# The attention's projections under a schedule written by hand, with the order of reads, split terms and unpacking fixed around their seven products

## The chip, the cores and the metric

The kernel runs on one core of a Trainium2 chip. The metric is the device time of one execution in microseconds (us). TensorE (PE) multiplies, with its weight loads shown apart (PEld). VectorE (DVE), ScalarE (ACT) and GpSimd (POOL) do the elementwise work. SyncE (SP), ACT and POOL issue DMA transfers. Each engine works through its own queue in order.

## The reference

The input is normalised, and the normalised rows feed two branches: causal attention with rotary positions, and a gated feed-forward network whose weights are 4-bit integers with a scale and a zero per group of 128 rows. The output is the input plus the attention's result times the SiLU of the feed-forward's result. There are 2 batches of 1024 tokens, 1024 features, 32 query heads and 8 key/value heads of 32 features, and 2752 inner features. All values are fp32.

```python
def reference(x, wq, wk, wv, wo, qweight_gu, qzeros_gu, scales_gu, g_idx_gu,
              qweight_down, qzeros_down, scales_down, g_idx_down):
    xn = layernorm(x)                                     # eps 1e-5
    q, k, v = heads(xn @ wq, 32), heads(xn @ wk, 8), heads(xn @ wv, 8)
    q, k = rope(q), rope(k)                               # pairs (0::2, 1::2), theta 10000
    k, v = repeat(k, 4), repeat(v, 4)
    scores = einsum('bqhd,bkhd->bhqk', q, k) / sqrt(32) + causal_mask
    s = einsum('bhqk,bkhd->bqhd', softmax(scores), v).reshape(2, 1024, 1024) @ wo
    w_gu, w_d = dequant(qweight_gu, ...), dequant(qweight_down, ...)
    gate, up = split(xn @ w_gu, 2752)
    g = silu((silu(gate) * up) @ w_d)
    return x + s * g
# dequant: W[i, j] = scale[g[i], j] * (nibble(qw)[i, j] - (nibble(qz)[g[i], j] + 1))
```

## The kernel before

The first batch is normalised (`norm`), then each batch goes through `project` (queries, keys, values), `attend` and `project_out`; while the first batch's output projection runs, the second batch is normalised. The feed-forward network of both batches comes last (`ffn_in_order`). Two jobs run beside these stages as generators that are advanced one step at a time with `next(side, None)`. `look` belongs to the first batch's projections: it surveys scales, zeros and group indices, spreads the zeros over rows in DRAM (`zb_gu`, L218, and `zb_d`, L223, issued by ACT), and turns the scales (`scales_turned`). `unpack` turns packed weights into numbers in DRAM, one unit of 256 columns in four steps: loads by SP (L242, L244), DVE operations on `nib` (L258, L260, L263), conversions on ACT (L267), a store by POOL (L249). In the version before, units 0 to 7 of the gate and up weights are unpacked in the first output projection, 8 to 19 in the second batch's projections, and 20 and 21 with the down weights in the second output projection.

`project` forms five blocks of 256 output columns: keys (block 0), then queries (blocks 1 to 4). A block is a matrix product cut into two halves in tokens, in the summed dimension and in columns, and worked out as seven products of half-size pieces in place of eight. The weights' pieces are `wa`, `wb` and their differences (`quarters`, L397 to L400), those of the input are quarters of `xnT` and four sums `S` (L391) in the space of `oT`. `pair` writes the seven products (L431) in the order 1, 5, 2, 6, 3, 7, 4 over three PSUM banks, each read by the sums at L442, L447, L450, L451 and L457. Four results of a block are turned by `turn_heads` (rotary positions: DVE L407 and L409, POOL L410 and L411), split into a high and a low part (ACT L413, DVE L415) and stored by SP (L416, L417). The loop runs product 4 of a block behind product 1 of the next block.

`split_x` splits the normalised input the same way for the feed-forward (ACT L483, DVE L484, stores L485 and L486). `head` is the object `Maxima`: `keys()` and `queries()` load the stacks of head group 0 from the stored rotations (L594, 4 transfers, and L599, 16 transfers), and `rows()` yields 45 steps, each a product of queries and keys in one of two PSUM banks (L640, mask L634) with its row maximum on DVE (L650), then the shifts (L672 to L677) and their transposes (L685). `values` projects the values in eight tiles (L472, L475). `weights(i)` loads a block's query weights (L350), and `load_kv` the value weights (L356).

Before the change a scheduler orders the instructions of `project` on each engine, by priority in the order written and by a model of when each becomes ready; `tc.issue_after` holds some behind a rotation. `attend` has `tc.manual_schedule()`, under which every engine issues in the order in which the code writes its instructions. The names that the prediction uses: block i, its products 1 to 7, X for the end of product 5, and "step" for one yield of `rows()`.

## Time and profile before

| | us |
|---|---|
| median of 3 runs | 2316.39 (2315.3 to 2318.07) |
| the profiled execution | 2317.56 |
| its span | 2315.8 |
| PE, DVE, ACT, POOL busy in the span | 2228.9, 1501.8, 1144.4, 838.4 |
| first batch: first product of the projections to the attention's first score | 28.70 to 234.59 |
| second batch: the same | 678.77 to 873.96 |

In a row of the time order, the first number is the start in us from the span's start, the second the length, then the engine, the line, the operation and its tiles, and x the number of merged instructions; brackets hold the idle time before it and what ended it. "SPq" and "ACTq" are DMA issues in those engines' queues. An fp32 product of 512 columns leaves two records per weight tile, so a product of a block is eight records. A busy PE may still run below its peak, since its ends are modelled; the granted clock is given apart.

### The profile page before, as it was taken

To read this page: it belongs to the slowest core of one execution; us is meant where nothing else is said; L and a number is where in the kernel's file an instruction comes from. 1 tells how busy PE (TensorE), PEld (TensorE's weight loads), DVE (VectorE), ACT (ScalarE), POOL (GpSimd) and SP (SyncE) were. 2 spreads that over 40 slices of the span, in tenths; PEclk is the share of its full clock that TensorE was granted. 3 is DMA by queue.
4 is the path that set the end of the run, shared out by engine and by line. 5 is a ranking of instruction groups with operands and counts; after the bars stand their busy time and mean duration, and the time that the engine had idled before them with its cause. 6 is when DMAs were issued, how large, how long until landed. Compare 5 with 4: busy or idle time off the path is not lost.

```text
span 2315.8 us, 30821 instructions
## 1 busy us (share of the span) xinstructions
PE 2228.9 (96%) x11233; PEld 1529.2 (66%) x11233; DVE 1501.8 (65%) x2336; ACT 1144.4 (49%) x1839; POOL 838.4 (36%) x599
## 2 busy tenths in 40 slices
PE   6979999999998889999999999999999999999997
PEld 3445555555873455555548878888877888888875
DVE  8664577773336765777732367766877777777775
ACT  2102555544233324544542465555787655556875
POOL 2514667775135445777661100000234100001362
PEclk9969999999999999999999999999999999999999
DMA  6645313112477875122119632322746645333474
GB/s 191 193 145 192 85 46 85 45 48 69 141 225 218 256 231 131 46 65 64 46 38 319 222 82 55 82 77 60 264 151 221 183 132 143 91 81 102 138 233 148
DMA packets 262185, 309.52 MB, mean 134 GB/s; under 512 B 19147, under 2 KB 197707, under 8 KB 261880
## 3 DMA queue, kind: packets, MB, share of 16 engines
q1 hardware_dynamic: 245172, 260.62, 37.8%
q0 software_dynamic: 10752, 38.02, 5.3%
q10 hardware_dynamic: 6100, 8.82, 1.4%
q8 instruction: 91, 1.49, 0.3%
q14 instruction: 70, 0.57, 0.1%
HBM read 214.58 MB, written 97.03 MB: 135 GB/s over the span
## 4 chain that ended last, share of the span: by engine, by line
PE 77%; DVE 5%; POOL 5%; DMA 5%; issue 4%; ACT 2%; SPq 1%; ACTq 0%; POOLq 0%; DVEq 0%
PE acc L1284 27%; PE acc L1165 12%; PE s L640 7%; PE st L747 7%; PE ps_wo L966 6%; PE o L794 5%; PE ps L431 4%; PE l L812 3%; PE st L762 2%; DMA zt<-zb_d 2%; PE s L634 1%; POOL p L907 1%; PE ps_v L472 1%; POOL rot L410 1%; POOL rot L411 1%
## 5 line engine op out<-in xcount | busy, mean ns | idle before, releaser
L1284 PE MATMUL acc<-x,w 128*128 128x512 f32 x2752 | 639.9, 393 | 1.1 <-ACT gate L1255 0.9
L1284 PEld LDWEIGHTS acc<-x,w 128*128 128x128 f32 x2752 | 512.6, 188 | 120.0 <-DVE h L1257 7.2
L1054 DVE TENSOR_SCALAR acc<-acc,r_gu 128x1024 f32<-128x1024 f32 x301 | 389.1, 1293 | 166.1 <-PE acc L1284 164.7
L650 DVE TENSOR_REDUCE mx<-s 128x1 f32<-128x512 f32 (+3 forms) x672 | 385.0, 609 | 162.6 <-PE s L634 94.7
L772 ACT ACTIVATE p<-st 128x512 f32<-128x512 f32 (+3 forms) x768 | 315.1, 497 | 316.1 <-PE st L762 316.0
L1052 ACT ACTIVATE acc<-acc,r_gu 128x1024 f32<-128x1024 f32 x301 | 327.7, 1089 | 231.1 <-PE acc L1284 226.3
L1268 POOL TENSOR_TENSOR h_lo<-h,h_hi 128x512 fp32r<-128x512 f32 x78 | 100.3, 1287 | 805.7 <-PE acc L1165 588.2
L907 POOL TENSOR_TENSOR p<-p 128x2048 f32<-128x2048 f32 (+3 forms) x122 | 360.0, 2955 | 9.0 <-PE o L794 4.6
L1054 DVE TENSOR_SCALAR acc<-acc,r_d 128x512 f32<-128x512 f32 x320 | 241.6, 759 | 62.1 <-PE acc L1165 59.4
L1052 ACT ACTIVATE acc<-acc,r_d 128x512 f32<-128x512 f32 x320 | 211.0, 663 | 62.0 <-PE acc L1165 55.2
L966 PE MATMUL ps_wo<-oT,w_o 128*128 128x256 f32 x1024 | 232.1, 382 | 0.0
L1165 PE MATMUL acc<-h_lo,w 128*128 128x512 f32 (+1 forms) x576 | 228.9, 397 | 2.9 <-POOL h_lo L1268 2.6
L1165 PE MATMUL acc<-h_hi,w 128*128 128x512 f32 (+1 forms) x576 | 229.5, 398 | 0.7 <-ACT h_hi L1267 0.7
L966 PEld LDWEIGHTS ps_wo<-oT,w_o 128*128 128x128 f32 x1024 | 191.1, 190 | 40.9 <-issue 16.7
L794 PE MATMUL o<-p,v 128*32 128x512 f32 (+3 forms) x1536 | 162.9, 496 | 0.8 <-POOL p L775 0.8
L775 POOL TENSOR_SCALAR_AFFINE_SELECT p<-p 128x512 f32<-128x512 f32 x128 | 80.6, 637 | 160.6 <-ACT p L772 160.6
L640 PE MATMUL s<-kst,room 128*128 128x512 f32 (+3 forms) x384 | 130.5, 379 | 0.0
L1165 PEld LDWEIGHTS acc<-h_lo,w 128*128 128x128 f32 (+1 forms) x576 | 108.4, 188 | 30.7 <-POOL h_lo L1268 5.1
L1165 PEld LDWEIGHTS acc<-h_hi,w 128*128 128x128 f32 (+1 forms) x576 | 108.3, 188 | 30.6 <-issue 2.9
L747 PE MATMUL st<-room,kst 128*128 128x512 f32 (+3 forms) x384 | 119.2, 371 | 3.2 <-ACT p L772 3.2
L413 ACT CAST rot_hi<-rot 128x512 fp32r<-128x512 f32 x40 | 24.7, 617 | 177.2 <-POOL rot L411 139.0
L267 ACT ACTIVATE nf<-nib 128x1024 fp32r<-128x1024 uint8 (+2 forms) x68 | 68.2, 1040 | 88.7 <-DVE nib L263 41.3
(194 smaller groups left out, 2688.7 us busy)
## 6 DMA issues: line engine op xcount, KB each, us to landing
w<-ng SPq DMA_DIRECT2D x86, 512.0 KB
w<-nd SPq DMA_DIRECT2D x63, 512.0 KB
ng<-nf POOLq DMA_DIRECT2D x42, 512.0 KB, 6.3
room<-qs SPq DMA_DIRECT2D x160, 128.0 KB
x<-xs SPq DMA_DIRECT2D x32, 512.0 KB
qst<-qs SPq DMA_DIRECT2D x96, 128.0 KB
xt<-in_L_attn_x SPq DMA_DIRECT2D x16, 512.0 KB
w_qk<-in_L_attn_wq SPq DMA_DIRECT2D x16, 512.0 KB
```

The costliest lines, as they stand in the source:

```text
L640: nc.tensor.matmul(s[:, c * w : (c + 1) * w], q[j][:, qt * P : (qt + 1) * P], k[:, k0:k1], start=n == 1, stop=c == n - 1 and (n > 1 or not ...
L650: nc.vector.tensor_reduce(mx[:, at, js[0] : js[0] + n, k0 // TB], s[:, : w * n].rearrange("p (j t) -> p j t", j=n), AX.X, ALU.max)
L747: nc.tensor.matmul(s[:, q0:], kst[g][:, kt * P : (kt + 1) * P], stack[g][j][:, qlo + q0 : qlo + TB], start=True, stop=False,)
L772: nc.scalar.activation(p[:, j, q0:], st[j][:, q0:], AF.Exp, scale=1.0 / math.sqrt(HD))
L794: nc.tensor.matmul(o[HD * j : HD * (j + 1), q0:], v[:, kt, HD * g : HD * (g + 1)], p[:, j, q0:], start=(kt == 0), stop=last,)
L907: what(*args)
L966: self.last = nc.tensor.matmul(ps[:, c * self.BLK : (c + 1) * self.BLK], self.ws[c0 + c][:, g, :], self.oT[:, g, t0 : t0 + self.BLK], star ...
L1052: nc.scalar.mul(a, a, r)
L1054: nc.vector.tensor_scalar(a, a, r, None, ALU.mult)
L1165: nc.tensor.matmul(acc[c], w[:k, c * P : (c + 1) * P], ht[:k, :], start=(f == 0 and t == 0), stop=(t == 1), skip_group_check=(f > 0),)
L1268: nc.gpsimd.tensor_tensor(at[1][:k, :], h[:k, f, tok], at[0][:k, :].bitcast(F32), ALU.subtract)
L1284: nc.tensor.matmul(a[:, n, :], w[i][:, g * P : (g + 1) * P], xs[t][:, g, n * TB : (n + 1) * TB], start=(g == 0 and t == 0), stop=(t == 1), ...
```

## The change

`project` is put under `tc.manual_schedule()` and its instructions are written in a fixed order. The rotation's split and stores become a function `leave`, kept in a list and written one or two products later. After each product, `others()` writes the leaving rotations, one `split_x` of half a tile, and one step of the side job (before: three steps per rotation in the second batch, one in the first). The fourth weight term, on POOL, is written after product 4 of the block before. Steps of the row maxima stand at fixed places: nine per block from block 2, and three before each tile of the values. `head.keys()` and `head.queries()` are written behind product 5 of blocks 1 and 2, and the warm-up of Exp behind the last rotation. In `look`, the loads of all three parts come first, and the parts follow in the order scales and zeros, down scales and zeros, turned scales, spreading of zeros. The units of unpacking become 0 to 10 in the first output projection, 11 to 18 in the second batch's projections, and 19 to 21 with the down weights in the second output projection.

```diff
@@ survey: words, scale and idx are loaded ahead of a first yield
+        scale = pool.tile([P, 8 * w], F32, name=f"scale_{tag}")
+        nc.sync.dma_start(scale, sc.rearrange("g n -> (g n)").rearrange("(p w) -> p w", p=P))
+        idx = pool.tile([k, m], I32, name=f"idx_{tag}")
+        nc.sync.dma_start(idx, gi.rearrange("(p m) -> p m", p=k))
+        yield
...
@@ scales_turned
+        by_g = pool.tile([G_D, D], F32, name="by_g")
+        nc.sync.dma_start(by_g, sc_d)
+        yield
...
         nc.vector.tensor_copy(l_gu, ps[:, :, :, G_GU - 1 :])
-        by_g = pool.tile([G_D, D], F32, name="by_g")
-        nc.sync.dma_start(by_g, sc_d)
+        yield
...
@@ look
-        yield from survey(pool, bad, sc_gu, qz_gu, gi_gu, z_gu, 0, "gu")
-        yield from survey(pool, bad, sc_d, qz_d, gi_d, z_d, 2, "d")
+        parts = [
+            survey(pool, bad, sc_gu, qz_gu, gi_gu, z_gu, 0, "gu"),
+            survey(pool, bad, sc_d, qz_d, gi_d, z_d, 2, "d"),
+            scales_turned(pool, psp),
+        ]
+        for part in parts:
+            next(part)
+            yield
+        for part in parts:
+            yield from part
+        yield
...
-        yield
-        scales_turned(pool, psp)
         yield
@@ project
-        ) as vps, tc.tile_pool(name="x_split", bufs=2, reuse_waits="tile") as xp:
+        ) as vps, tc.tile_pool(name="x_split", bufs=2, reuse_waits="tile") as xp, tc.manual_schedule():
...
-                t = [wp.tile([P, H, P], F32, name=f"t_{i}") for i in range(3)]
+                t = [wp.tile([P, H, P], F32, name=f"t_{i}") for i in range(2)]
                 nc.vector.tensor_tensor(t[0], wb[:, low], wa[:, low], ALU.subtract)
                 nc.vector.tensor_tensor(t[1], wb[:, high], t[0], ALU.subtract)
                 nc.gpsimd.tensor_tensor(wb[:, low], wb[:, high], wb[:, low], ALU.subtract)
-                nc.gpsimd.tensor_tensor(t[2], wa[:, high], t[1], ALU.subtract)
...
+                yield B
+                B[4] = wp.tile([P, H, P], F32, name="t_2")
+                nc.gpsimd.tensor_tensor(B[4], wa[:, high], t[1], ALU.subtract)
+                yield B
...
+                nc.gpsimd.tensor_tensor(t1, t1, t2, ALU.add)
+
+                def leave():
+                    hi = pool.tile([P, TB], F32R, name="rot_hi")
+                    nc.scalar.copy(hi, t1)
+                    lo = pool.tile([P, TB], F32R, name="rot_lo")
+                    nc.vector.tensor_tensor(lo, t1, hi.bitcast(F32), ALU.subtract)
+                    nc.sync.dma_start(dst[0, :, tok], hi.bitcast(F32))
+                    nc.sync.dma_start(dst[1, :, tok], lo.bitcast(F32))
+
+                leaving.append(leave)
+
+            leaving, splits = [], []
+
+            def others(n=1):
+                while len(leaving) > n:
+                    leaving.pop(0)()
+                if splits:
+                    splits.pop(0)()
+                next(side, None)
...
-                        if s % 2 and i > 1:
+                        if i not in (1, 5) and (s == 1 or s == 3 and i != 4):
                             next(work, None)
...
                 product(5, S[0], 2, True)
                 nc.scalar.copy(p5, banks[2])
                 nc.gpsimd.tensor_tensor(p5, p1, p5, ALU.add)
+                others(0)
                 yield
                 product(2, A[0, 1], 0, False)
                 turn_heads(banks[0], 0, dsts[0])
+                others()
                 yield
                 product(6, S[1], 1, True)
                 nc.vector.tensor_tensor(u2, banks[1], p1, ALU.add)
+                others(0)
...
-            B = quarters(*loads[0])
+            make = quarters(*loads[0])
+            B = next(make)
+            for s in sums:
+                nc.vector.tensor_tensor(*s)
+            next(make)
...
                 next(g)
                 for _ in running or ():
-                    pass
+                    next(make)
+                next(g)
+
                 if i == 1:
+                    head.keys()
                     w = load_kv(None, wv, w_k)
+                if i == 2:
+                    head.queries()
                 if 0 < i < PAIRS - 1:
                     loads.append(weights(i + 1))
-                for _ in range(4):
+                if i:
+                    splits += [lambda c=c, n=n: split_x(c, n) for c in (2 * i - 2, 2 * i - 1) for n in range(NB)]
+                for _ in range(3):
                     next(g)
                 if i + 1 < PAIRS:
-                    B = quarters(*loads[i + 1])
+                    make = quarters(*loads[i + 1])
+                    B = next(make)
                 next(g)
                 running = g
-            for _ in running:
-                pass
+            next(running)
+            others(0)
+
+            warm = tp.tile([P, 1], F32, name="warm")
+            nc.scalar.activation(warm, eps, AF.Exp)

             for t in range(NT):
-                next(work, None)
+                for _ in range(3):
+                    next(work, None)
                 values(t)
+                others(0)
...
-                        side = unpack(up, range(8, 20), False)
+                        side = unpack(up, range(11, 19), False)
...
-            side = unpack(up, range(8) if b == 0 else range(20, NF), b == B - 1)
+            side = unpack(up, range(11) if b == 0 else range(19, NF), b == B - 1)
```

## The prediction

> **What bounds the kernel now.** I read the page first, then busy time by stretches, then the engines' instructions in order of time inside the two projections, and last the waits. Of the page, four rows matter.
>
> ```profile
> span 2315.8 us, 30821 instructions
> PE 2228.9 (96%) x11233; PEld 1529.2 (66%) x11233; DVE 1501.8 (65%) x2336; ACT 1144.4 (49%) x1839; POOL 838.4 (36%) x599
> ...
> PE   6979999999998889999999999999999999999997
> PEclk9969999999999999999999999999999999999999
> ```
>
> TensorE is busy in 96% of the span. Only three places fall short: slices 0 to 3 (the first batch's normalisation and projections), slices 12 to 14 (the second batch's projections) and the last slice. The change touches the first two alone, so the rest of the kernel is a fixed cost, and the question is what the two projections lose. The stretches give it (columns: PE, PEld, DVE, ACT, POOL busy, granted clock, DMA share, GB/s).
>
> ```profile
> 28.00:128.00 100.00, 95.48 (x280) 46.50 (x279) 72.29 (x131) 12.84 (x22) 43.40 (x32) 1.00 0.50 152
> 128.00:168.00 40.00, 26.45 (x66) 14.93 (x65) 28.76 (x58) 3.69 (x8) 3.80 (x3) 0.57 0.42 132
> 168.00:234.00 66.00, 62.04 (x185) 35.64 (x186) 31.15 (x55) 13.06 (x25) 23.92 (x18) 0.95 0.56 202
> 679.00:768.00 89.00, 77.77 (x173) 33.48 (x171) 57.14 (x91) 25.67 (x34) 48.52 (x40) 0.94 0.71 214
> 768.00:874.00 106.00, 93.05 (x320) 55.60 (x318) 72.36 (x145) 28.29 (x45) 43.14 (x37) 0.98 0.75 236
> ```
>
> Between 128 and 168 us TensorE works 26 of 40 us, at 0.57 of its clock: the first batch's hole. No engine is full anywhere; these stages are lost to waits. TensorE in order of time gives the length of each projection and two restarts.
>
> ```profile
> 28.70 3.60 PE L431 MATMUL ps<-xnT,w_kv 128*128 128x512 f32 x8
> ...
> 193.90 5.40 PE L431 MATMUL ps<-xnT,w_qk 128*128 128x512 f32 x8 [3.27 <-ACT p L447]
> ...
> 234.59 1.29 PE L747 MATMUL st<-room,room 128*128 128x512 f32 x4
> ```
>
> The first projection runs from 28.70 to 234.59, where the first score of the attention (L747) starts: 205.9 us. The second runs from 678.77 to 873.96: 195.2 us. The row at 193.90 also shows what a pause costs beyond itself: after 3.27 us idle, eight records take 5.40 us instead of 3.60, so 1.8 us more. What must be done is less. A product is eight records, 3.43 us from start to start; 35 of them make 120.1. The value projections are 128 records at 0.2175, 27.8. The row maxima of head group 0 cost 0.29 us for 384 columns (at 776.84 the step with two product records takes 1.15 until 777.99, two records are 0.86); 18,432 columns are 48 times that, 13.9. Sum 161.8. So the two projections lose 44.1 and 33.4 us. Now who waits: ACT in the hole, then SP (the DMA issuer) and TensorE in the second batch.
>
> ```profile
> 115.93 30.97 ACTq L223 DMA_DIRECT2D zb_d<-z_d  x19
> 146.94 0.62 ACT L413 CAST rot_hi<-rot 128x512 fp32r<-128x512 f32 x1 [30.42 <-DMA zb_d<-z_d]
> ```
>
> ```profile
> 750.07 1.41 SPq L417 DMA_DIRECT2D qs<-rot_lo  x1
> ...
> 753.29 12.62 SPq L599 DMA_DIRECT2D room<-qs  x16
> ```
>
> ```profile
> 762.12 0.80 PE L640 MATMUL s<-room,room 128*128 128x128 f32 x2
> ...
> 767.62 0.62 PE L640 MATMUL s<-room,room 128*128 128x128 f32 x1
> ```
>
> ACT issues 19 of the 21 copies zb_d in one run of 31 us, and a rotation's split stands behind them for 30.42 us. In the second batch the loads of query group 0 (16 of them) follow the store of the last rotation, and the maxima's last head starts at 767.62, 17.5 us after that store was issued. In the old order TensorE filled that gap with products.
>
> **The change, part by part.** Under the manual schedule every engine issues in the order written, so I follow that order. The waits it is to remove (DVE's rot_lo on ACT's rot_hi, 39.1 us over 15 times in the second projection, now deferred by a stage or two) are part of the 44.1 and 33.4 us above; I start from 161.8 and add what the written order makes each engine wait for. Block i's stages on TensorE are product 1 of i, product 4 of i-1, then 5, 2, 6, 3, 7 of i.
>
> 1. Queries before the maxima. head.queries() is written behind product 5 of block 2, and the first maxima step stands inside product 2 of the same block, 1.7 us later. TensorE queues everything behind it: the rest of product 2 and all that follows. Let X be the end of product 5. Product 4 of block 1 ended at X-3.4; its sum, rotation and shuffle (0.7, 0.68, 0.72) and POOL's two multiplies (1.27 each, L410, L411) end at X+1.4, ACT's split at X+2.0, the low half's at X+2.7. Then the store must land. Trace: issued 750.07, landed 756.68, 6.6 us. The Trainium skill, "DMA: Bandwidth & Descriptors", section "Anatomy of one DMA — SWDGE (gpsimd) path", fits a fixed 2.0 us and the bytes at 436 GB/s: 2.6 us for these 256 KB (estimate; it is stated for POOL's queue and this store is SP's). Beside the unpacking traffic I take the row. Then 15 loads end at 765.91, 9.2 us, and the last lands 1.7 later. TensorE resumes at X+20.2: a stop of 18.5 us, plus 1.8 for the restart; with the rule it would be 14.5. SP stands at the first of these loads meanwhile; behind it are the weights of block 3, wanted only after the gap.
> 2. Keys and weights. keys() behind product 5 of block 1 puts two key loads, the load of wv and the next query weights behind a store: 2.7 + 6.1 (the key store at 717.86) + 0.9 + 0.4 + 1.2 (two at 0.64), then 4.9 to land (132.10): X+16.2, wanted at X+13.7. About 3 us in the second batch, none in the first, where stores land in 3 (70.12 to 73.24).
> 3. Second batch, counted from 678.77. Block 0 and the first two own stages of block 1 with product 4: nine products, 30.9; one block 24.0; stall 3: X = 57.9. Gap and restart 22.0. Remaining 19 products less the 1.7 done, 63.5; values 27.8; maxima 13.9. That is 185.1 if DVE keeps up. DVE per block: four rotations with their low halves 7.3, sums 2.4, x_lo 2.4, two terms 1.2, nine maxima 5, a shift 1.9, unpacking 1.9: 22.1 of 26.8 us. Here a rule speaks against the change: "SBUF — State Buffer", "Who interferes with whom", has a DVE operation with two SBUF inputs and a POOL read of SBUF shut each other out for a whole instruction. Ten such DVE operations per block against 14 us of POOL in 26.8 would lose about ten times 0.52 times half of 1.27, 3.3 us. The row has rot_lo at a mean of 0.80 against its shortest 0.675: ten times 0.125, 1.3. I take the row; both fit under 26.8. But three maxima steps now stand together before each value tile with two banks between them: the third waits for a read, 0.7 us (read 0.69 behind a step of 0.29), six times: 4. The two shifts are followed at once by their transposes, about 2 each (2.65 at 167.95): 4. In-order waits of DVE for ACT or a landed x_lo (8.6 us at 797.62) in three blocks: 0 to 12, I take 5. Sum 198.1 against 195.2: +2.9.
> 4. First batch. DVE works off terms 2.2, four sums 9.2, then six rotations 7.8, seven sums 4.6, five low halves 3.3, x_lo 2.0, four terms 3.6 and the look's 18.0 (its lines between 39.83 and 57.3, and 94.36 to 99.7), with some 6 of waits: the sum that frees product 4 of block 1 comes at 85.7, so X is 93. The copies zb_gu (8 at 0.48, 3.8) now stand on ACT after product 1 of block 2, and all 21 zb_d one stage later, ahead of the split that the queries need. Issue is 0.5 to 1.0 each in the trace (six in 5.33 at 141.57); at 0.75, 15.8. ACT is free at 107.4 instead of about 92; p5 0.6, split 0.6, low half 0.7, store 0.4 and 3 to land, loads 9, landing 1.7: 123.5. Restart 1.8. Then 63.5 + 27.8 + 13.9, and DVE terms 4 + 4 + 2: 240.5 against 234.6, +5.9. With zb_d at 0.5 it is 5 less, at 1.0 it is 5 more.
> 5. Unpacking moved. Three units go to the first output projection, which hides them: its last splitting (L267) ends at 664, TensorE's last product at 678.8, a unit takes about 5.5 (646.73 to 652.24); without the cover, +5; I take +1. One goes to the second, where twelve units take 49 us (1254.82 to 1303.49), 4.1 each, and the last split stands 10 us ahead of the feed-forward: between 0 and +5, I take +3.
> 6. The Exp warm-up now runs behind the last rotation. The table loads of 1.28 at 235.37 and 874.35 go: -2.6. The look's loads up front and POOL's term split off: nothing, since DVE's sums hold block 0 and POOL is busy 29.8 us of the first 64; without that cover, 0.4 per load on SP and 1.3 per term.
>
> Sum: 2.9 + 5.9 + 1 + 3 - 2.6 = +10.2. The profiled execution took 2317.56 (span 2315.8), 1.2 over the median of the three runs, 2316.39; from the median this gives 2326.6.
>
> **The rivals.** *Faster.* The same gap before the first maxima, but short: place block 2 of both batches, price what TensorE stands still. If stores land in 3 us in the second batch too, its gap is 15 for 18.5 and the wait for weights (3) goes; with zb_d at 0.5 and the loads at their median of 0.42, the first gap is 23 for 30.5; if the reads keep up, only the 4 us of third steps stay in each batch, 9 and 6 less. That is 29 less in all: -18.8, about 2298. It decides by the sum of gaps, weights and DVE terms: I have 75; under 65 the change is not slower, under 60 it is faster. For it: the gaps in the old order (44.1 and 33.4 lost) are closed otherwise, and DVE has 22.1 of 26.8. Against it: 6.6 us to land, and 30.97 of issue.
> *No difference.* Gap paid and old waits saved cancel within 4.6 us (0.2%, about what a measurement of this kernel can tell from no change), or the planned order was in effect the written one.
> *DVE becomes the bound.* Twelve in-order waits make each of three blocks 31 us, not 26.8, in both batches: 25 in place of my 7, about 2345. For it: x_lo waits of 2.4 us and POOL collisions; against it: DVE busy 129.5 of 195 us in the second projection.
>
> **How the numbers follow.** Forecast 0.50 (2319 to 2340), faster 0.28, no difference 0.14, DVE bound 0.08. Slower by over 0.2%: 0.50 + 0.08 = 0.58; same 0.14; faster 0.28. The range leaves out the far end of the faster case and of the DVE case: 2294 to 2346.
>
> **What would show it.** Right: TensorE idle for 15 us or more before the first L640 step of each batch, released by the loads of room from qs; in the first batch a run of about 20 zb_d issues on ACT ending just before that split; attention starting near 240 and, from its projection's start, after 198 us. Steps 5 and 6: a feed-forward start up to 3 us later behind the second output projection, and no table load at L772. Wrong: the first maxima step starts without a pause, or the holes are there and the projections still end 10 us early, in which case the waits saved were worth more than the 33 and 44 less my terms.

## The result and the profile after

The changed kernel takes 2380.31 us (median of 4 runs, 2379.58 to 2384.9) against 2316.12 for the kernel before on the same chip: ratio 1.028, 95% interval 1.0262 to 1.0298. It is 64 us slower. The direction was foreseen, the size was not: the forecast was 2326.6 and the range ended at 2346.

The rows of its page that answer to those of before:

```profile
span 2377.6 us, 30830 instructions
PE 2230.1 (94%) x11233; PEld 1531.8 (64%) x11233; DVE 1525.9 (64%) x2336; ACT 1141.2 (48%) x1838; POOL 853.7 (36%) x599
...
PE   7578999999998688999999999999999999999997
PEclk9779999999999899999999999999999999999999
```

TensorE's busy time is what it was (2230.1, before 2228.9). The span grew, and it grew where the change is: slices 1 to 3 and 12 to 15. I cut each profiled execution at four points: the first product of a projection, and the first work of TensorE after that projection's last value product. That gives four stretches: first projection, attention and output projection of the first batch ("between"), second projection, and the rest.

| profiled execution | first | between | second | rest | span |
|---|---|---|---|---|---|
| before | 205.9 | 444.2 | 195.0 | 1442.0 | 2315.8 |
| after | 237.9 | 442.7 | 228.6 | 1439.6 | 2377.6 |
| difference | +32.0 | -1.5 | +33.6 | -2.4 | +61.8 |

The whole loss lies in the two projections, about half in each. By stretches (columns: us, PE, PEld, DVE, ACT, POOL busy, clock, DMA share, GB/s):

```profile
28.00:101.00 73.00, 64.54 (x167) 29.28 (x167) 58.78 (x109) 9.69 (x17) 30.66 (x22) 0.91 0.34 114
101.00:140.00 39.00, 6.58 (x14) 2.88 (x13) 2.24 (x4) 2.24 (x4) 4.25 (x4) 0.54 0.75 212
140.00:219.00 79.00, 74.56 (x200) 35.72 (x200) 61.73 (x106) 14.15 (x25) 41.98 (x28) 0.97 0.59 198
219.00:267.00 48.00, 38.19 (x164) 31.55 (x165) 15.00 (x31) 5.33 (x11) 3.47 (x3) 0.89 0.28 84
711.00:790.00 79.00, 60.83 (x130) 24.90 (x128) 52.40 (x68) 20.11 (x29) 41.43 (x35) 0.96 0.68 214
```

From 101 to 140 us TensorE works 6.6 of 39 us, VectorE and ScalarE 2.2 each (ScalarE's DMA issues are not counted as work): everybody waits. What for is told by TensorE's instructions in order of time,

```profile
88.08 6.56 PE L448 MATMUL ps<-xnT,w_qk 128*128 128x512 f32 x8
...
97.90 3.60 PE L448 MATMUL ps<-oT,t 128*128 128x512 f32 x8
126.14 0.19 PE L240 MATMUL ps_bad<-ones_f,one 128*1 128x1 f32 x2 [24.64 <-DVE one L238]
...
131.86 0.45 PE L666 MATMUL s<-room,room 128*128 128x128 f32 x1 [1.39 <-DMA room<-qs]
...
139.88 3.72 PE L448 MATMUL ps<-xnT,w_qk 128*128 128x512 f32 x4
```

and by ScalarE's:

```profile
85.82 0.61 ACT L504 CAST x_hi<-xnT 128x512 fp32r<-128x512 f32 x1
100.26 0.58 ACT L464 COPY p<-ps 128x512 f32<-128x512 f32 x1 [13.83 <-DVE rot L415]
100.28 5.05 ACTq L230 DMA_DIRECT2D zb_gu<-z_gu  x8
105.70 0.62 ACT L421 CAST rot_hi<-rot 128x512 fp32r<-128x512 f32 x1 [4.86 <-DMA zb_gu<-z_gu]
105.73 17.69 ACTq L235 DMA_DIRECT2D zb_d<-z_d  x21
123.45 0.58 ACT L468 COPY p<-ps 128x512 f32<-128x512 f32 x1 [17.14 <-DMA zb_d<-z_d]
```

Read it from top to bottom. ScalarE is idle 13.83 us before it copies product 1 into p1. Some 8 of these go by until product 1 itself ends, at 94.6 (the row at 88.08). The last 5.6 are spent until VectorE has shuffled product 4 of the block before: that rotation still reads the old p1, and p1 has one buffer. Only then come the eight zb_gu, the 21 zb_d, and behind those the rotation's split that the query store needs. TensorE meanwhile stands at the small product of the look (ps_bad), whose input on VectorE is queued behind that split.

In the second batch the stop before the first maxima is as forecast, 19 us:

```profile
784.62 0.80 PE L660 MATMUL s<-mask_q,ident_r 128*128 128x512 f32 x1
796.63 0.44 PE L666 MATMUL s<-room,room 128*128 128x128 f32 x1 [11.21 <-DMA room<-qs]
...
803.62 3.72 PE L448 MATMUL ps<-xnT,w_qk 128*128 128x512 f32 x4
```

But X, the end of product 5 ahead of it, comes 72.6 us after the projection's start and not 57.9. Two rows of VectorE show the longest of what came before it:

```profile
728.28 0.52 DVE L268 TENSOR_SCALAR nib<-qw 128x512 uint16<-128x512 uint16 x1 [9.55 <-DMA qw<-in_L_ffn_qweight_gu]
...
771.51 0.69 DVE L506 TENSOR_TENSOR x_lo<-xnT,x_hi 128x512 fp32r<-128x512 f32 x1 [8.10 <-ACT x_hi L504]
```

Unpacking's first load comes late and VectorE, in order, waits 9.55 us for it with sums and rotations behind; later it waits 8.10 us for a half of x whose buffer is still being stored.

### The profile page after: what moved, and what is told of

It is laid out like the page before. It is cut to its first block, busy times and chain, and to the rows that moved or that the text cites. A ratio compares the mean times of both kernels' runs of the same rounds, so it can differ in the third digit from the quotient of the medians.

```text
span 2377.6 us, 30830 instructions
## 1 busy us (share of the span) xinstructions
PE 2230.1 (94%) x11233; PEld 1531.8 (64%) x11233; DVE 1525.9 (64%) x2336; ACT 1141.2 (48%) x1838; POOL 853.7 (36%) x599
## 4 chain that ended last, share of the span: by engine, by line
PE 78%; DVE 5%; POOL 5%; issue 5%; DMA 4%; ACT 2%; SPq 1%; ACTq 1%; POOLq 0%; DVEq 0%
PE acc L1310 26%; PE acc L1191 11%; PE ps_wo L992 8%; PE s L666 7%; PE st L773 7%; PE o L820 5%; PE ps L448 4%; PE l L838 3%; PE ps_v L496 3%; PE st L788 2%; PE s L660 1%; POOL p L933 1%; DMA ng<-nf 1%; DVE mx L676 1%; ACT p L798 1%
## 5 line engine op out<-in xcount | busy, mean ns | idle before, releaser
L1080 DVE TENSOR_SCALAR acc<-acc,r_d 128x512 f32<-128x512 f32 x320 | 241.6, 759 | 62.1 <-PE acc L1191 59.7
L1078 ACT ACTIVATE acc<-acc,r_d 128x512 f32<-128x512 f32 x320 | 210.9, 663 | 61.8 <-PE acc L1191 54.9
L1191 PEld LDWEIGHTS acc<-h_lo,w 128*128 128x128 f32 (+1 forms) x576 | 108.6, 189 | 30.6 <-POOL h_lo L1294 5.2
L1191 PEld LDWEIGHTS acc<-h_hi,w 128*128 128x128 f32 (+1 forms) x576 | 108.4, 188 | 30.5 <-issue 2.9
L416 POOL TENSOR_TENSOR rot<-rot,cs 128x512 f32<-128x512 f32 x40 | 60.2, 1504 | 150.7 <-DVE rot L415 149.0
```

The lines of the kernel that those rows point to most:

```text
L1078: nc.scalar.mul(a, a, r)
L1080: nc.vector.tensor_scalar(a, a, r, None, ALU.mult)
L1191: nc.tensor.matmul(acc[c], w[:k, c * P : (c + 1) * P], ht[:k, :], start=(f == 0 and t == 0), stop=(t == 1), skip_group_check=(f > 0),)
```

## The experiments

Theory W: the 64 us are waits in the written order, each at a place that can be named, and a repair of the place returns it. Rival D: VectorE has become the bound (the prediction's last rival), so repairs only move the waiting. Rival O: the new order itself is bad, strict or not. The us are medians of whole kernels; the stretches, cut as above, are of the one profiled execution. The ratio is to the kernel before on the same chip.

| run | us | ratio, 95% interval | first | second | rest |
|---|---|---|---|---|---|
| e1_no_manual | 2329.1 | 1.0059 (1.0041 to 1.0078) | 196.7 | 218.7 | 1439.7 |
| e2_late_rows | 2364.2 | 1.0204 (1.0187 to 1.0221) | 226.1 | 222.3 | 1442.0 |
| e3_zb_spread | 2370.2 | 1.0228 (1.0209 to 1.0248) | 224.8 | 228.9 | 1445.5 |
| e4_p1_two | 2368.2 | 1.0227 (1.0210 to 1.0244) | 227.7 | 226.2 | 1439.8 |
| e5_units | 2380.7 | 1.0271 (1.0254 to 1.0288) | 238.9 | 222.8 | 1449.7 |
| e7_last_later | 2376.1 | 1.0252 (1.0236 to 1.0267) | 234.9 | 226.8 | 1444.2 |
| e8_x3 | 2375.8 | 1.0241 (1.0222 to 1.0260) | 234.1 | 230.7 | 1439.7 |
| e10_weights_first | 2390.0 | 1.0310 (1.0293 to 1.0327) | 241.6 | 236.4 | 1439.9 |
| e14_zb_p1 | 2363.5 | 1.0212 (1.0198 to 1.0226) | 222.4 | 225.4 | 1440.0 |
| e6_all | 2323.6 | 1.0026 (1.0016 to 1.0037) | 204.0 | 196.6 | 1451.1 |
| e16_strict_early | 2343.4 | 1.0119 (1.0103 to 1.0136) | 214.2 | 215.4 | 1438.4 |
| e12_strict_repaired | 2317.4 | 1.0003 (0.9994 to 1.0012) | 204.8 | 199.9 | 1439.7 |
| e13_before_units | 2326.9 | 1.0044 (1.0031 to 1.0057) | 205.4 | 206.8 | 1439.6 |
| e9_free_held | 2326.5 | 1.0049 (1.0032 to 1.0066) | 196.1 | 212.7 | 1441.3 |
| e11_free_repaired | 2311.1 | 0.9977 (0.9969 to 0.9985) | 187.7 | 207.1 | 1439.0 |
| e15_side_held | 2312.9 | 0.9981 (0.9974 to 0.9987) | 205.4 | 187.2 | 1442.0 |
| e17_second_held | 2293.0 | 0.9894 (0.9878 to 0.9911) | 186.9 | 188.2 | 1444.6 |
| e18_more_units | 2292.7 | 0.9896 (0.9880 to 0.9913) | 188.5 | 190.2 | 1438.7 |

The stretch between was 442.6 to 444.1 in all but e15_side_held (447.5). The rest moved between 1438.4 and 1445.5 among kernels with the same units in it, so a few microseconds there say nothing.

**e1_no_manual: order or strictness?**

```
-        ... as xp, tc.manual_schedule():
+        ... as xp:
```

> The changed kernel without the manual schedule in the projections: the same written order is handed to the scheduler, which may move instructions of one engine past each other. Theory W (waits): the 64 us are in-order waits at named places (row maxima behind query loads, the p1 copy and what lies behind it on ScalarE, nib on VectorE behind a late load); a scheduler that may move work past them gets most of it back: both batches' projections 195 to 215 us long instead of 237.9 and 228.6, total 2316 to 2340. Rival O (the order itself): the written order gives the wrong work first, and with no strictness the first instructions still stand in front; the total stays within 10 us of 2380. Rival D (VectorE has become the bound: 137.8 and 143.7 us busy in the two projections, against 132.2 and 129.5 before): total stays above 2365, and VectorE's idle time shrinks little.

The first projection came out at 196.7, 9 under the kernel before and 41 under the changed one; so the written order is not bad in itself, and rival O falls. TensorE's rows show with what the scheduler closes the hole:

```profile
97.27 3.19 PE L496 MATMUL ps_v<-w_kv,xnT 128*128 128x256 f32 x14
...
107.16 4.05 PE L496 MATMUL ps_v<-w_kv,xnT 128*128 128x256 f32 x18
...
123.91 5.41 PE L448 MATMUL ps<-oT,w_qk 128*128 128x512 f32 x8 [9.28 <-ACT p L468]
```

Value products, which need only wv and x, go ahead at 97 us; in the changed kernel the first stands at 226. The second projection missed its 195 to 215, with a new stop of 30.6 us at its start: splits of x ran ahead of the four sums (L521) on VectorE.

**e2_late_rows, e3_zb_spread, e4_p1_two: one repair of a stop each.** Row maxima one block later (e2); the zb copies later and in twos (e3); a second buffer for p1 (e4).

```
-   g = pair(B, dsts, work if i > 1 else iter(()))
+   g = pair(B, dsts, work if i > 2 else iter(()))
...
-   for _ in range(3):          # ahead of each value tile
+   for _ in range(4):
```

> Row maxima begin in block 3, not 2, and four steps go ahead of each value tile instead of three. Theory W: the stop of TensorE before the first maxima in the second batch (784.6 to 803.6, 19 us) goes, and some 8 to 12 us of it come back as 14 maxima steps more in the value tiles, which VectorE reads one after another: -7 to -12 there. In the first batch the stop shrinks only to the end of the copy of p5 behind zb_d (123.45, then the query stores): TensorE goes on with products 2 and 6 of block 2 but these need p5's bank: -5 to -15. Total 2352 to 2368. Rival D: what the stop loses comes back entirely in the tail; total within 5 us of 2380.

```
-        yield                  # ahead of zb_gu
+        for _ in range(4):
+            yield
...
+            if g % 2:           # in both loops, zb_gu and zb_d
+                yield
```

> The issues of zb_gu (8) and zb_d (21) begin four side steps later and go two to a step, instead of 8 and 21 in one piece. Theory W: in the first batch ScalarE's 22.7 us of issues no longer stand in one block ahead of the split of the queries; the stop of TensorE before the first maxima (101.4 to 139.9 with four steps between) falls from 38 to 18 to 22 us; the second batch, which has no such issues, stays within 2 us of 228.6. Total 2358 to 2366. Rival: the ScalarE issues are late only because of p1's single buffer (13.8 us), or because the queries' stores land late anyway; then the stop stays over 30 us and the total over 2372.

```
-   p1, p5, u2 = part("p1"), part("p5"), part("u2")
+   p1 = pool.tile([P, TB], F32, name="p1", bufs=2)
```

> p1 has two buffers instead of one, so that ScalarE's copy of product 1 does not wait until product 4 of the block before is turned. Theory W: waits of the p1 copy on the rotation of L415 (40.5 us in 4 in the first batch, longest 13.8; 32.0 us in 4 in the second) go; in the first batch zb_gu is issued 10 to 13 us earlier, so the queries split and TensorE resumes 8 to 12 us earlier; the second batch gains 2 to 6 us (products that wait for ScalarE's p1, 5.9 us in all). Total 2362 to 2372. Rival: the copy's wait is covered by something else that ends at the same time (VectorE's in-order queue); total within 4 us of 2380.

All three got shorter. The second batch's stop is gone in e2, yet it got only 6.3 us back: TensorE waited 7.92 for weights instead, and the value part takes 42.9 us for 39.1. In e3 the stop fell as expected (TensorE goes on at 121, not 139.9) and the first projection by 13; the total missed by 4, and the rest of the profiled execution ran 5.9 longer, which is within that stretch's spread. In e4 the first projection lost 10.2 us, as expected. Its copy of product 1 goes as soon as the product ends:

```profile
93.05 0.59 ACT L465 COPY p<-ps 128x512 f32<-128x512 f32 x1 [8.00 <-PE ps L448]
```

Of the 10 us, 6 come off the stop, 3 off what follows it, and under 2 off the time to X.

**e14_zb_p1: both repairs of the first batch.**

> The changed kernel with two repairs of the first batch together, zb issues spread and p1 with two buffers; each alone took 13.1 and 10.1 us off the first batch's 239.2. If the two are one chain (p1's copy holds ScalarE, then the issues of zb hold it further), together they take 20 to 24 us and TensorE stops in the first batch for as long as in the second, 19 to 22 us: total 2350 to 2358. If they overlap (each alone leaves the same next wait): 13 to 15 us, total 2362 to 2367.

222.4: together 15.5 us and not 23. They overlap, because behind both stands the same next wait, the queries' own store and load, which stops TensorE for 17 us (20 in the second batch).

**e5_units, e10_weights_first, e7_last_later, e8_x3: smaller suspects alone.** Units 0 to 7, as before, in the first output projection, 8 to 15 in the second batch's projections and 16 on in the second output projection (e5), weights ahead of keys and queries on SP (e10), the last rotation not left at once (e7), three buffers for the split of x (e8).

```
-   side = unpack(up, range(11, 19), False)
+   side = unpack(up, range(8, 16), False)
-   ... range(11) if b == 0 else range(19, NF) ...
+   ... range(8) if b == 0 else range(16, NF) ...
```

> The units of unpacking go back to the ranges of before: 8 in the first output projection, 8 in the second projection (12 before), the rest in the second output projection. Theory W: the second batch's first load of qw no longer waits for memory that the last unit of the first output projection gives back, so VectorE's wait of 9.55 us at 728.28, and TensorE's of 4.04 us behind it, go: second projection 228.6 to 220 to 224 us; the second output projection carries 3 units more, +0 to +3. Total 2373 to 2378. Rival: that load is late because of SP's own order, not because of memory, and the wait stays; total within 3 us of 2380.

```
    if i == 1:
+       loads.append(weights(2))
        head.keys()
...
    if i == 2:
+       loads.append(weights(3))
        head.queries()
```

> On SP the loads of weights(2) and weights(3) stand ahead of those of keys and queries, which wait there for stores to land. Theory W: the waits of TensorE on w_qk (2.10 us in the second batch of the changed kernel) and of products 5 and 6 on p (3.38 us, through x_lo) shrink; the query gap stays (its loads come 1 to 2 us later): second batch -2 to -5, first 0 to -2; total 2374 to 2380. Rival: nothing but these loads waits there; within 3 us of 2380.

```
    next(running)
-   others(0)
```

> The last rotation of a batch is not left at once after product 4 but with the first value tile's step. Theory W: VectorE's rot_lo no longer stands ahead of the first maxima reads of the tail, where TensorE waited 5.27 and 6.49 us: both waits fall to 2 us or less, total 2370 to 2374. Rival (the reads are late because VectorE is behind with three steps per tile in any case): within 3 us of 2380.

```
-   tc.tile_pool(name="x_split", bufs=2, ...)
+   tc.tile_pool(name="x_split", bufs=3, ...)
```

> The split of x has three buffers instead of two. Theory W: ScalarE's waits of x_hi on the stores (15.0 us in 3 in the second batch, longest 9.35) go, and with them VectorE's x_lo wait of 8.1 us and TensorE's 3.4 us on p5 behind it: second batch -3 to -5, total 2374 to 2378. Rival (the stores wait on SP behind the key loads, so a third buffer only fills as well): within 3 us of 2380.

e5: the wait for the first qw is gone and the second projection is 5.8 shorter, as expected; but three units more in the last output projection cost 10 us (1449.7 against 1439.6; 1451.1 in e6_all), not 0 to 3. e10 is a miss, 10 us slower. TensorE's two waits of 2.10 and 3.38 us became one of 8.67 on p5, and the queue behind it is that of the changed kernel, only longer: ScalarE's x_hi has no buffer, VectorE's x_lo stands in front of the terms of the next block.

```profile
775.71 0.62 ACT L504 CAST x_hi<-xnT 128x512 fp32r<-128x512 f32 x1 [10.56 <-DMA xs<-x_hi]
```

```profile
776.40 0.69 DVE L506 TENSOR_TENSOR x_lo<-xnT,x_hi 128x512 fp32r<-128x512 f32 x1 [9.32 <-ACT x_hi L504]
...
777.67 0.68 DVE L400 TENSOR_TENSOR t<-w_qk 128x512 f32<-128x512 f32 x1
```

Why the stores of x land later there was not separated. e7 returned 3.0 and 1.8 us and missed its total by 2: the reads that waited 5.27 and 6.49 us then waited 1.42 and 2.66, so theory W has the place right, but the reads after them waited 1.3 us longer in each batch. e8 met its total, but not for the reason given: the second projection did not get shorter, its wait on p5 became a wait for weights (5.95 us). Of the small repairs none is worth much alone.

**e6_all, e12_strict_repaired, e16_strict_early: the repairs together, still strict.** e6 joins e2, e3, e4, e5, e7, e8 and e10. e12 is e6 with units 0 to 7, 8 to 18, and 19 on. e16 is e12 with the maxima in block 2 and three steps to a tile again.

> All repairs at once, still under the manual schedule: row maxima from block 3 with four steps to a value tile, zb issues spread, p1 with two buffers, units in the ranges of before, three buffers for the split of x, the last rotation left later, and the loads of weights(2) and weights(3) ahead of those of keys and queries on SP. Theory W: each named stall goes and its cover is enough: -34 to -48 of the first and second batch together, total 2332 to 2346, still slower than before since the value tiles take 43 to 45 us for 39. Rival D (VectorE the bound, and in-order reading of the late maxima): total over 2352. Rival E (the strict order costs only these waits): total under 2325.

> All the repairs under the manual schedule once more, but with units 0 to 7 in the first output projection, 8 to 18 in the second projection and 19 on in the last. With units 8 to 15 and 16 on, the last output projection took 1451.1 us to the end against 1439.6 in the changed kernel: three units there cost 11.5 us. Theory (a unit in the last output projection costs 3.8 us, one in the second projection under the manual schedule under 2): total 2312 to 2318, within 0.2% of before. Rival (in the second projection three units under a strict order cost as much): 2320 to 2326.

> The repaired strict order (2317.4) with the row maxima in block 2 again and three steps to a value tile, all other repairs kept. Theory W: the stop before the first maxima is back, 17 to 20 us in both batches, and the values' 4 to 6 us per batch and the later maxima's waits are saved: +10 to +14 per batch, total 2336 to 2346. Rival (with the other repairs the queries come early enough): stop under 10 us, total under 2330.

e6 was better than theory W gave (2332 to 2346) and falls to rival E: against the kernel before, the strict order costs these waits and hardly more. e12 is the settling run. With every instruction still issued in the written order it is level with the kernel before, 1.0003, so nearly all of the 64 us goes with these repairs. VectorE is busy 147.7 of 200 us in its second projection, more than the 143.7 of 228.6 in the changed kernel, and so was not the bound: rival D falls. e16 sizes the query stop, with the place of the maxima, when all else is repaired: 26 us, within theory W's total. In its second batch

```profile
742.16 0.80 PE L666 MATMUL s<-mask_q,ident_r 128*128 128x512 f32 x1
759.87 0.45 PE L672 MATMUL s<-room,room 128*128 128x128 f32 x1 [16.91 <-DMA room<-qs]
...
766.68 3.26 PE L452 MATMUL ps<-xnT,w_qk 128*128 128x512 f32 x4
```

the stop lasts from 743 to 766.7. X falls 55.8 us after the projection's start at 685.05, near the prediction's 57.9. The stop is longer than expected (17 to 20) and longer than in the changed kernel: here, as in e10, the weights go ahead of the queries on SP. So the 26 us are not exactly what the stop costs in the changed kernel.

The ladder, by ratios times 2317: changed kernel +65; zb and p1 repaired +49; with units, x buffers, weights and last rotation +28; with the maxima a block later +1. The third step's 21 us are not split further; the runs of its parts alone (e5, e7, e8, e10) do not add up to it.

**e13_before_units: the moved units alone, in the kernel before.**

> The kernel before, with the ranges of units of the change alone: 11 in the first output projection (8 before), 8 in the second projection (12), the rest in the last (one more). Prediction's step 5: +1 to +5 for the first output projection, +3 for the last, and the second projection freed of four units gains little: 2316 to 2324. Rival (the moved units are what makes the second batch start late under any order, since their memory comes free late): 2325 to 2335.

+10 us, above all that step 5 allowed for, and not where step 5 looked. The output projections are unchanged (between 444.1, rest 1439.6); the second projection takes 206.8 for 195.0. SP's queue tells where it begins. In the kernel before, the weights of block 1 are issued as the projection begins:

```profile
675.78 4.52 SPq L350 DMA_DIRECT2D w_qk<-in_L_attn_wq  x4
```

With three units more ahead, the first load of the second unpacking waits for a store of the first to land (columns: total, times, longest), and the weights go out behind it:

```profile
SPq L242 <- DMA ng<-nf: 18.4, 1, 18.4
```

```profile
689.30 1.47 SPq L242 DMA_DIRECT2D qw<-in_L_ffn_qweight_gu  x2
...
694.20 4.99 SPq L350 DMA_DIRECT2D w_qk<-in_L_attn_wq  x4
```

It is not for these weights that TensorE stops, but for ScalarE:

```profile
694.15 0.43 ACTq L979 DMA_DIRECT2D sT<-wo_r  x1
694.69 0.58 ACT L447 COPY p<-ps 128x512 f32<-128x512 f32 x1 [11.59 <-DMA qw<-in_L_ffn_qweight_gu]
```

```profile
695.33 6.46 PE L431 MATMUL ps<-xnT,w_kv 128*128 128x512 f32 x8 [10.61 <-ACT p L447]
```

The copy of product 1 stands in ScalarE's queue behind a store of the output projection (L979), and that store goes out only at 694.15. The profile puts the wait down to the late loads of qw; why the store would wait for them it does not show.

**e9, e11, e15, e17, e18: without strictness, to a faster kernel.** e9 is e1 with each split of x held behind the last rotation that left. e11 adds the second p1, the spread zb, and units 0 to 7, 8 to 18 and 19 on. e15 also holds the side steps (look and unpacking), at first behind the last sum and the load of weights(1). e17 holds them in the second batch alone. e18 is e17 with units 8 to 19 in the second projection. The lines are e17's.

```
    with ExitStack() as held:
        for r in recent:         # last rotation's split (at first: last sum, weights(1))
            held.enter_context(tc.issue_after(r.ins))
        if splits:
            splits.pop(0)()
        if b:
            next(side, None)
    if not b:
        next(side, None)
```

> Without the manual schedule, and each split of x held behind the last rotation that left (its ScalarE and VectorE instructions). Without the manual schedule alone, the 16 splits of the second batch ran ahead into the first output projection, with two buffers and stores between them, and the four sums stood behind them on VectorE: TensorE stopped 30.6 us behind L521. Theory W: that stop goes, the second projection takes 186 to 194 us instead of 218.7, the first stays at 195 to 200; total 2296 to 2308, faster than before. Rival: the splits, held back, come in the way of the maxima reads again, and the gain is 15 us or less: total 2312 to 2325.

> No manual schedule, splits of x held behind the last rotation that left, and three repairs: p1 with two buffers, zb issues spread over the side steps, units 0 to 7 in the first output projection, 8 to 18 in the second projection, 19 on in the last. Theory W: the stop behind L525 in the second batch (16.24 us, VectorE behind a unit's load that waits for memory of the first output projection's units) goes, the p5 copy behind zb_d (10.25 us in the first batch) goes, waits on the p1 copy (6.82 and 3.18) shrink: 2326.5 - 16 - 9 - 5 = 2292 to 2304, faster than before. Rival: what these stops free is taken by VectorE, busy for 67% of the projections; total 2305 to 2318.

> The free order with the repairs (2311.1), and the side steps (look and unpacking) held behind the sums, the load of weights(1) and later the last rotation that left, as the splits are. Theory W: in the second batch unpacking no longer stands ahead of the sums on VectorE (6.87 us of stop) and of weights(1) on SP; waits of TensorE on u (6.41, 6.98, 4.82) shrink: total 2292 to 2304. Rival (held units only move to the maxima and values): 2308 to 2316.

> The two free orders joined: in the first batch the steps of the look run free (first projection 187.7 us with them free, 205.4 held), in the second batch those of unpacking are held behind sums, weights(1) and the last rotation (187.2 held; free 196.6 and a stop of 6.87 before it). Theory W: the two gains are independent, since they lie in different batches: 215.7 + 447.5 + 187.2 + 1442 = 2288 to 2298. Rival (holding also changes the splits' place in the first batch and loses it): 2306 to 2314.

> The same with units in the ranges of before: 8 to 19 in the second projection and 20 on in the last output projection, one unit moved from there. Theory (a unit in the last output projection costs 3.8 us, one in the second projection 1 to 2): 1 to 3 us below the kernel with 8 to 18. Rival: the second projection's VectorE and ScalarE have no room for it: 1 to 4 us above.

e9 gained 3 us, not 20: in front of the sums there now stood a unit's nib, waiting for its load (a stop of 16.24 us). e11 is 6 us under the kernel before and ended in its rival's range: its first projection fell to 187.7, the second kept late loads. e15 missed too, since what it won in the second (187.2) it gave back in the first (205.4), where the look's steps are better free. e17 has both, 186.9 and 188.2, and the total that its theory gave: 24 us faster than before. e18 is the same to 0.3 us, so which of the two stages has the one unit makes no difference that these runs can tell. The page of e17:

```profile
span 2292.3 us, 30824 instructions
PE 2217.8 (97%) x11233; PEld 1524.0 (66%) x11233; DVE 1510.5 (66%) x2336; ACT 1143.6 (50%) x1839; POOL 842.4 (37%) x599
...
PE   6999999999998999999999999999999999999997
```

Slices 1 to 3, which were 5, 7 and 8 in the changed kernel and 9, 7 and 9 before, are all 9.

## Why the prediction was wrong in size

The mechanism was right as far as it went: strict order, TensorE behind query loads, ScalarE behind its DMA issues. What failed is terms left at nothing (the single buffer of p1 in step 4, the late release behind the moved units in step 5, the wait for the buffers of x before X) and one term too small (VectorE in step 3). The profiled span grew by 61.8, where I had 10.2. Each projection splits into the time to X (in the second from the projection's start, in the first from the span's), the time from X until the products go on, and what follows, with the slow restart in it:

| | forecast | measured | short by |
|---|---|---|---|
| second: to X | 57.9 | 72.6 | 14.7 |
| second: from X until the products go on | 20.2 | 21.6 | 1.4 |
| second: from there to the attention | 120.0 | 134.4 | 14.4 |
| first: to X | 93.0 | 101.4 | 8.4 |
| first: from X until the products go on | 30.5 | 38.5 | 8.0 |
| first: from there to the attention | 117.0 | 126.8 | 9.8 |

That is 56.7 us short in the two projections, and 5 too many in the other two stretches.

- **Step 1 (queries before maxima)** held: forecast X+20.2, measured X+21.6. Inside, its terms are off and cancel. The chain that ended last shows them (start, length, what; the pieces left out are the other loads' issues):

```profile
787.48 5.55 DMA qs<-rot_lo
793.03 0.02 issue
793.05 0.32 SPq L625
...
799.44 3.80 DMA room<-qs
```

 The low half's store was issued at X+5.4, not X+2.7, because VectorE had other steps in front. The first load that reads it waited 5.55 us for 6.6, the 15 loads were issued in 6.8 us for 9.2, and the last took 3.80 to land for 1.7. The rule weighed there, of the Trainium skill's "DMA: Bandwidth & Descriptors" ("Anatomy of one DMA — SWDGE (gpsimd) path"), gives an estimate of 2.6 us for the store, so the row of before was nearer.
- **Step 2 (weights behind keys)**: forecast 3 us in the second batch. TensorE waited 2.10 for w_qk, and 3.38 more for p5 behind the x_lo row shown above. Right in size as far as the weights go; the two buffers of x, which wait for their stores, were put at nothing before X (step 3 prices such waits only in the three blocks behind it). Moving the loads did not help (e10).
- **Step 4 (first batch) failed.** I put zb_gu on ScalarE right behind product 1, and overlooked that the copy in front of it writes p1, which product 4 of the block before still reads. The buffer count was there to be read in the code. It held ScalarE for 5.6 us behind product 1, so that zb_gu began 4.1 us later, counted from X, than forecast. The issues, with a split between them, took 3.5 us more than forecast (the 21 zb_d 17.69 us, 0.84 each for my 0.75). These two make up 7.6 of the stop's 8.0. Before X the same buffer held TensorE for 3.94 us in block 1:

```profile
64.29 6.50 PE L448 MATMUL ps<-xnT,w_qk 128*128 128x512 f32 x8 [3.94 <-ACT p L464]
```

 e4 and e14 show what the buffer is worth: 10 us alone, 15.5 with the zb copies. The rest of the first batch's 26 us is explained only in part: TensorE stood 4.32 us before the look's products at 87.14, and waited 14 us in the tail, where I had 10.
- **Step 5 (units moved) failed.** I asked what hides the three units inside the first output projection and found cover. The cost was in the next stage: a store of the last units landing late, the next units' load late, and behind it ScalarE's copy of product 1 (e13: TensorE waited 10.61 us, the second projection took 11.8 more) or, in the written order, VectorE's sums (e5: 5.8). The 5.8 are over a third of the 14.7 us that the second batch missed before X. The +4 that step 5 put on the two output projections was not seen: the stretch between and the rest shrank.
- **Step 3's VectorE terms (13 us) were too small.** In the tail of the second batch TensorE waited as follows.

```profile
PE s L666 <- DVE mx L676: 9.7, 8, 6.5
PE m_ps L711 <- DVE mt L700: 6.4, 2, 3.8
PE ps L448 <- ACT p L464: 2.6, 2, 1.7
PE ps L448 <- DVE p L459: 2.5, 2, 1.8
```

 Together 21.2 us (columns: total, times, longest): 8 more than my terms. The other 6 of the 14 were not separated; after such a wait the records are slow for a while. e16 has the same tail, 133.7 us, with all other repairs in place, so it goes with the order of maxima and products.
- **Step 6 (warm-up)**: the stretch between is 1.5 us shorter, and the rest 2.4, for the 2.6 forecast. The two table loads are gone from the attention's start, as forecast; the rest's spread is larger than 2.6, so what that is worth is not settled.
- **The rivals.** VectorE as the bound named about 2345, also 35 us short, and not the cause: in the second projection the engine was busy 143.7 of 228.6 us and waited in order. *Faster* was out because not one of its conditions, short gaps, no wait for weights and reads that keep up, came true.

What stays open: why e10 delayed the stores of x, the 6 us of the second batch's tail and what step 4 leaves unexplained in the first, why ScalarE's store waited in e13, and why the look's steps cost 17.7 us in the first batch when held (e15).

## What to carry to other kernels

In a hand-written order, price each instruction by what it must still wait for when its turn comes: for every tile with one buffer, find its last reader of the round before, and put everything behind the writer on that engine's bill. Work that is well hidden where it is moved to can still return its memory or its queue late, so follow its last release into the next stage. Keep independent work (here the value products) free to fill, and pin only the few instructions that got in the way: with that and the repairs, the same products took 87 us less than in the strict order, and 24 less than in the repaired strict order of e12.

## What was not expected of the hardware

The stop costs more than its length: in both batches the four records right behind it took 3.72 us, where four take 1.93 undisturbed. In the 39 us of the first batch's stop the granted clock was 0.54, and in the second batch 0.84 over the 60 us from 790 to 850, where TensorE stood idle for 18.6:

```profile
790.00:850.00 60.00, 41.41 (x110) 20.07 (x111) 37.91 (x64) 12.20 (x18) 22.34 (x17) 0.84 0.72 210
```

Behind a wait of 3.80 us at 810.08 in e16, four records took 3.31 us. So several short waits, each with its restart, cost more than their sum in the list of waits.
